# The last transformer stack of a fused kernel: the squared halves of each query and key head added on VectorE, half as many norm products on TensorE, and a new order of the stack's steps

## The chip, the cores and the metric

The kernel runs on one core of one Trainium2 chip. The metric is the device time of the whole kernel in microseconds, the median of several runs. The core's engines have short names in the profile: PE is TensorE, PEld its weight loads, DVE is VectorE, ACT is ScalarE, POOL is GpSimd, and SPq is the queue from which SyncE issues DMAs.

## The reference

The input is 16 sequences of 256 tokens with 128 features. Four blocks follow one another: an attention block with 16 heads, a mixture of low-rank experts, a retention block, and then a stack of six identical layers. The change touches the stack alone. One layer of it, with what matters for the change:

```
qkv = shift_tokens(x) @ Wqkv                     # 16 heads of 64
q = l2norm(q) * q_scale;  k = l2norm(k) * k_scale    # l2norm(t) = t / max(|t|, 1e-12)
q = q * cos * scale + rotate_half(q) * sin * scale   # k alike, with 1 / scale
out = local_attention(q, k, v)      # windows of 32 tokens, each sees itself and the one before
x = out @ Wo + x
x = feed_forward(shift_tokens(x)) + x     # layer norm, W1, a * gelu(gate), W2
```

The length |t| of a head needs the sum of 64 squares. The kernel holds a head as two halves of 32 features ("both parts of a head").

## The kernel before, in words

The work of the stack is cut into 96 units: unit u is layer u // 16 and sequence u % 16. The feed-forward block and what belongs to it (`fn`, `nat`, `st`, `rs`, `z`, `trf`, `fz`, `fg`, `gl`, `fa`, `fh`, `fy`, `xsf`) works on two sequences at once and so exists for even units alone. All data is float32.

One unit goes through these steps; the line is where the method begins. G counts four groups of four heads, k is 0 for queries and 1 for keys, and hu, tt and i count halves and quarters of the sequence or of the heads.

- `pqk.G.k` (L913, PE): two products of 128 by 256, the two halves of the heads, into a PSUM tile with two buffers (`ps_qk`).
- `sq.G.k` (L923, ACT) squares them into the SBUF tile `sq` of the group, which has four buffers. The tile is (128, k, half, 256).
- `t2.G.k` (L929) and `rot.G.k` (L934), both DVE, multiply the same PSUM tile by the rotary tables. `add.G` (L939, POOL) adds the two, 128 by 1024 elements.
- `nr` (L945, PE): the sums of squares. A fixed 0/1 matrix `gather` sums over the 32 features of a half in the partitions; the product runs over eight blocks b of 32 tokens, two halves hf, and four groups G, and accumulates the two halves in PSUM. In two parts of 32 products it makes 64 products for a unit. A float32 product is two instructions, so 128 matmul instructions.
- `rnA`, `rnB`, `rnC` (L961 to L968; DVE, ACT, DVE): maximum, square root, reciprocal.
- `bcD` (L973, SPq): one DMA stores the 128 by 64 result to DRAM, and eight more read it back, spread over the partitions, into the tile `bc` (one buffer).
- `norm.G` (L986, POOL): the group, 128 by 1024, times `bc`.
- `pv.i` (L991, PE), `vc.i` (L1002, ACT), `vs.tt` (L1005, SPq): the values, their copy out of PSUM, and four DMAs that copy them to a second place in SBUF. `vs.0` reads what `vc.0` and `vc.1` wrote, and `vs.1` what `vc.2` and `vc.3` wrote.
- `s.hu.tt.gh` (L1017, PE): scores of the groups G = 2 gh and 2 gh + 1. They lie in one PSUM tile (`ps_s`, one buffer) for the four steps of a hu; the next hu can be written once `sm.hu` has read it.
- `sm`, `mx` (DVE), `sub` (POOL), `exp` (ACT), `su`, `rec` (DVE): the softmax, L1043 to L1078.
- `pt`, `pTc`, `o`, `on`, `ot`, `oTc`, `y`, `xsu`: transposes, products with the values, and the output projection.

PSUM tiles of `pt`, `ot`, `pv`, `fg`, `fa`, `fn`, `trf`, `fy`, `y` and `nr` share one pool with two buffers (`misc`, L906): such a step waits until the tile two steps before it has been read.

The order of issue is written out by hand in the string `ORDER` (L1283). A word such as `norm.0:2` is a step and an offset d. The loop at L1343 runs a period j over all words and issues each for unit u = 2j + d where that unit exists. So a period holds every step twice, once for an even and once for an odd unit (feed-forward steps once); the 96 units make 48 periods, and a few more at both ends fill and empty the pipeline. Each engine works through its own steps strictly in this order, and so does SPq. Weights of the next layer are loaded by `follow` (L1315), which puts a DMA on SPq right behind the step that triggers it: the query and key weights of group G behind the second `pqk` of that group for sequence 15, the rotary tables behind the first `t2` of sequence 7, the value weights behind the first `pv` of sequence 9, the output weights behind the second `y` of sequence 15, the feed-forward weights behind `fy` of sequence 14. The query-key, output and feed-forward weights have one buffer, so that their DMA waits until that step has run. In the last layer `rs` also issues a DMA of the residual (`kept`), and `xsf` adds a transpose on PE, an addition on DVE and the DMA of the result.

Of the kernel before, what the change touches and what calls it, by code (L numbers as in the profile page):

```python
# [13 lines left out]
ALU = mybir.AluOpType  # L14
# [15 lines left out]
DEPTH, H2, D2, WIN = 6, 16, 64, 32  # L30
# [81 lines left out]
def kernel(ctx: ExitStack, tc: tile.TileContext, a: dict, widths: dict, out: bass.AP):  # L112
    nc = tc.nc
# [730 lines left out]
    gather = c["gather"].rearrange("p (b m) -> p b m", b=8)  # L844
# [43 lines left out]
    class Unit:  # L888
# [9 lines left out]
        def tile(self, pool, shape, what, *n, tag=None, **kw):  # L898

            key = (what, *n)  # L900
            if key not in self.tiles:
                name = f"{what}{self.u}_" + "".join(map(str, n))
                self.tiles[key] = pool.tile(shape, F32, tag=tag or what, name=name, **kw)
            return self.tiles[key]

# [35 lines left out]
            nc.gpsimd.tensor_tensor(to, to, self.t_2(G), ALU.add)  # L941

        def nr(self, part):  # L945
            nr = self.misc("nr")[:, 0:64]
            for b in range(4 * part, 4 * part + 4):
                for hf in range(2):
                    for G in range(4):
                        nc.tensor.matmul(  # L950
                            nr[32 * G : 32 * G + 32, :],
                            lhsT=gather[:, b, :],
                            rhs=self.squares(G)[:, :, hf, WIN * b : WIN * b + WIN],
                            start=(b == 0 and hf == 0),
                            stop=(b == 7 and hf == 1),
                        )

        def r_n(self):
            return self.tile(s2, [P, 64], "rn")
# [194 lines left out]
    class Forward(Unit):  # L1154
# [126 lines left out]


    ORDER = """  # L1283
        nr.0:2 t2.2.0:2 rot.2.1:2 y.1:-1 exp.1:0 sm.0:1 nr.1:2 t2.2.1:2 xsu:-1 pqk.0.1:3 add.3:2 rnA:2 rnB:2 pt.1.0:0
        s.1.0.0:1 su.1:0 rnC:2 add.2:2 rec.1:0 sq.0.1:3 fy:-4 s.1.1.0:1 mx.0:1 t2.0.1:3 rot.0.1:3 pqk.1.1:3 pTc.1.0:0
        sq.1.1:3 pt.1.1:0 o.0.0:0 xsf:-4 pqk.0.0:3 sub.0:1 pTc.1.1:0 fn:-2 t2.1.1:3 rot.1.1:3 t2.0.0:3 o.1.0:0 nat:-2
        exp.0:1 rot.0.0:3 bcD:2 pqk.1.0:3 add.0:3 on.0:0 sq.0.0:3 norm.0:2 pv.0:1 st:-2 s.1.1.1:1 norm.1:2 pv.3:1
        pqk.2.0:3 s.1.0.1:1 t2.1.0:3 vc.0:1 vc.3:1 ot.0.0:0 sq.1.0:3 pv.1:1 rot.1.0:3 rot.2.0:3 rs:-2 t2.2.0:3
        oTc.0.0:0 o.0.1:0 pt.0.0:1 sm.1:1 vc.1:1 sq.2.0:3 pqk.3.0:3 ot.0.1:0 sq.3.0:3 pTc.0.0:1 s.0.0.0:2 pqk.2.1:3
        z:-2 add.1:3 mx.1:1 trf:-2 rot.3.0:3 t2.3.0:3 oTc.0.1:0 su.0:1 sub.1:1 o.1.1:0 fz:-2 vs.0:1 pv.0:2 pqk.3.1:3  # L1290
        sq.2.1:3 on.1:0 t2.2.1:3 s.0.1.0:2 pv.3:2 vc.0:2 pt.0.1:1 norm.2:2 norm.3:2 exp.1:1 t2.3.1:3 vc.3:2 rot.2.1:3
        rot.3.1:3 vs.1:1 o.0.0:1 ot.1.0:0 oTc.1.0:0 rec.0:1 pTc.0.1:1 pqk.1.0:4 s.0.0.1:2 pt.1.0:1 add.2:3 su.1:1
        t2.1.0:4 sq.3.1:3 pqk.1.1:4 nr.0:3 pTc.1.0:1 nr.1:3 ot.1.1:0 rnA:3 rnB:3 rnC:3 fg.0:-2 bcD:3 sq.1.0:4
        oTc.1.1:0 gl.0:-2 s.0.1.1:2 sm.0:2 y.0:0 s.1.0.0:2 y.1:0 sq.1.1:4 s.1.1.0:2 xsu:0 rec.1:1 pt.1.1:1 pTc.1.1:1
        mx.0:2 rot.1.0:4 add.3:3 fa.0:-2 o.1.0:1 fg.1:-2 sub.0:2 t2.1.1:4 pqk.0.1:4 exp.0:2 fh.0:-2 rot.1.1:4
        s.1.0.1:2 t2.0.1:4 gl.1:-2 pv.1:2 pqk.3.1:4 on.0:1 s.1.1.1:2 ot.0.1:1 add.1:4 rot.0.1:4 vc.1:2 rot.3.1:4
        ot.0.0:1 sq.0.1:4 sq.3.1:4 oTc.0.1:1 norm.2:3 oTc.0.0:1 t2.3.1:4 pqk.0.0:4 sq.0.0:4 o.0.1:1 rot.0.0:4 norm.1:3
        sm.1:2 fa.1:-2 norm.3:3 pv.2:2 fh.1:-2 t2.0.0:4 o.1.1:1 pqk.3.0:4 sq.3.0:4 fg.2:-2 s.0.1.1:3 vc.2:2 norm.0:3
        gl.2:-2 vs.0:2 t2.3.0:4 on.1:1 pv.2:3 fa.2:-2 vc.2:3 s.0.0.1:3 add.0:4 pt.0.0:2 vs.1:2 fh.2:-2 pqk.2.0:4
        rot.3.0:4 ot.1.0:1 rot.2.0:4 pTc.0.0:2 oTc.1.0:1 su.0:2 s.0.0.0:3 rec.0:2 mx.1:2 sub.1:2 pqk.2.1:4 pt.0.1:2  # L1300
        ot.1.1:1 sq.2.1:4 pTc.0.1:2 s.0.1.0:3 y.0:1 sq.2.0:4 oTc.1.1:1
    """.split()

    weights = {}
# [4 lines left out]
    for word in ORDER:  # L1309
        name, d = word.split(":")  # L1310
# [105 lines left out]
```

## Time and profile before

| | |
|---|---|
| median of 3 runs | 4457.3 us (4455.6, 4457.3, 4475.08) |
| the profiled execution's own time | 4461.62 us |
| its span | 4459.9 us |
| busy in the span: PE, DVE, ACT, POOL | 4177.4, 2847.6, 2124.0, 2483.0 us |
| mean granted TensorE clock | 0.947 of full speed |

The profile is one execution. Busy shares are means over the whole span. The stack begins with its first weight load at 774 us and takes the rest. A stretch from one `fy` to the next is one period of the order, and the view of busy time by windows gives each engine's busy time in such a stretch. The timeline lists instructions in order of time: start, duration, engine, line, operation, what is written and read, the number of instructions merged into the row, and in brackets how long the engine stood idle before it and what released it.

### The profile page before, as it was taken

How to read it: one execution, taken by the hardware profiler on the slowest of the kernel's cores; microseconds unless marked ns; L12 is line 12 of the kernel's file. 1: busy time of each engine (PE TensorE's matmuls, PEld its weight loads, DVE VectorE, ACT ScalarE, POOL GpSimd, SP SyncE). 2: the span in 40 equal slices, each digit the busy share in tenths (PEclk: the TensorE clock that was granted, in tenths of full speed). 3: DMA queues.
4: the chain of work that ended last, by engine and by line, in shares of the span. 5: the costliest groups of instructions: out<-in, count | busy, mean ns of one | idle time of the engine just before them, and what ended most of it. 6: DMA issues, size and time to landing. Idle time of an engine off the chain costs nothing.

```text
span 4459.9 us, 219983 instructions
## 1 busy us (share of the span) xinstructions
PE 4177.4 (94%) x101856; PEld 2842.7 (64%) x101856; DVE 2847.6 (64%) x5628; ACT 2124.0 (48%) x3387; POOL 2483.0 (56%) x1419
## 2 busy tenths in 40 slices
PE   5888896799999999999999999999999999999998
PEld 3655664566666666666666666666666666666655
DVE  4555543567666666766667676766676766666664
ACT  2434432345555555545455455554555554544443
POOL 2433333666666666666666565665565665655552
PEclk9889876899999999999999999999999999999999
DMA  3200000222222222222222222222222222222221
GB/s 113 79 27 22 13 6 21 66 69 65 60 60 62 62 67 66 53 67 65 68 62 60 65 62 72 58 62 66 58 67 67 62 57 67 66 66 54 52 67 40
DMA packets 208917, 261.08 MB, mean 59 GB/s; under 512 B 54143, under 2 KB 164605, under 8 KB 207101
## 3 DMA queue, kind: packets, MB, share of 16 engines
q1 hardware_dynamic: 204796, 243.38, 22.1%
q8 instruction: 799, 13.09, 1.3%
q10 hardware_dynamic: 3200, 3.62, 0.3%
q14 instruction: 122, 0.99, 0.1%
HBM read 140.98 MB, written 17.83 MB: 36 GB/s over the span
## 4 chain that ended last, share of the span: by engine, by line
PE 81%; DVE 5%; issue 4%; DMA 3%; POOL 3%; SPq 2%; ACT 2%; ACTq 0%; POOLq 0%; DVEq 0%
PE pqk L916 15%; PE s L1028 12%; PE pv L994 8%; PE o L1104 6%; PE pt L1083 4%; PE ot L1129 4%; PE fa L1234 3%; PE fg L1221 3%; PE st L271 2%; SPq L981 2%; POOL qk L988 1%; PE sa L230 1%; PE or L537 1%; PE oa L306 1%; PE sr L510 1%
## 5 line engine op out<-in xcount | busy, mean ns | idle before, releaser
L941 POOL TENSOR_TENSOR qk<-qk,t 128x1024 f32<-128x1024 f32 x384 | 907.2, 2373 | 307.0 <-DVE qk L935 208.8
L1059 POOL TENSOR_TENSOR sm<-sm,mx 128x1024 f32<-128x1024 f32 x192 | 365.1, 1902 | 1005.8 <-DVE mx L1055 711.3
L916 PE MATMUL pqk<-xs,wqk 128*128 128x256 f32 x3072 | 861.3, 404 | 15.7 <-DVE qk L935 4.6
L1028 PEld LDWEIGHTS s<-qk 32*32 32x32 f32 x49152 | 535.4, 104 | 407.4 <-issue 334.6
L924 ACT ACTIVATE sq<-pqk 128x512 f32<-128x512 f32 x768 | 459.7, 599 | 631.6 <-PE pqk L916 543.4
L1028 PE MATMUL s<-qk 32*32 32x64 f32 x49152 | 666.4, 224 | 69.0 <-POOL qk L988 59.7
L930 DVE TENSOR_TENSOR t<-pqk,rot 128x512 f32<-128x512 f32 x768 | 522.5, 684 | 275.0 <-ACT sq L924 136.7
L916 PEld LDWEIGHTS pqk<-xs,wqk 128*128 128x128 f32 x3072 | 538.4, 194 | 246.3 <-issue 87.3
L935 DVE TENSOR_TENSOR qk<-pqk,rot 128x512 f32<-128x512 f32 x768 | 516.9, 683 | 268.1 <-PE s L1028 137.5
L994 PE MATMUL pv<-wv,xs 128*64 128x512 f32 x1536 | 429.4, 638 | 0.0
L1091 ACT COPY pT<-pt 128x512 f32<-128x512 f32 x384 | 224.4, 584 | 375.6 <-PE pt L1083 337.3
L1104 PEld LDWEIGHTS o<-v,pT 64*32 64x32 f32 x24576 | 273.1, 107 | 173.5 <-issue 161.9
L1104 PE MATMUL o<-v,pT 64*32 64x64 f32 x24576 | 339.6, 227 | 7.8 <-issue 5.5
L1003 ACT COPY v<-pv 128x512 f32<-128x512 f32 x384 | 223.9, 583 | 239.6 <-PE pv L994 239.4
L1044 DVE TENSOR_TENSOR sm<-s,c_ident 128x1024 f32<-128x1024 f32 x192 | 233.6, 1217 | 58.2 <-PE s L1028 58.2
L286 POOL TENSOR_SCALAR_AFFINE_SELECT pe<-pe 128x512 f32<-128x512 f32 x128 | 81.6, 638 | 328.1 <-ACT pe L279 311.6
L1083 PE MATMUL pt<-c_ident,sm 128*128 128x128 f32 x1536 | 244.8, 282 | 0.8 <-ACT oT__71843 L1135 0.8
L1129 PE MATMUL ot<-c_ident,on 128*128 128x128 f32 x1536 | 234.0, 280 | 1.4 <-ACT f_gl L1227 0.8
L1067 DVE TENSOR_REDUCE su<-sm 128x16 f32<-128x1024 f32 x192 | 230.1, 1198 | 1.5
L1063 ACT ACTIVATE sm<-sm 128x1024 f32<-128x1024 f32 x192 | 203.3, 1059 | 57.1 <-POOL sm L1059 56.0
L1055 DVE TENSOR_REDUCE mx<-sm 128x16 f32<-128x1024 f32 x192 | 226.0, 1177 | 0.1
L242 DVE CUSTOM_DVE_ANT_0 junk<-sa,c_mask 128x128 f32<-128x128 f32 (+1 forms) x512 | 181.9, 355 | 64.6 <-PE sa L230 31.5
(2243 smaller groups left out, 6740.9 us busy)
## 6 DMA issues: line engine op xcount, KB each, us to landing
v<-v SPq DMA_DIRECT2D x576, 128.0 KB
v<-v SPq DMA_DIRECT2D x192, 64.0 KB
rot_l<-in_rot_dram SPq DMA_DIRECT2D x12, 512.0 KB
rot<-rot_l SPq DMA_DIRECT2D x12, 512.0 KB
wqk<-in_wqk_dram SPq DMA_DIRECT2D x24, 256.0 KB
rot<-rot SPq DMA_DIRECT2D x6, 1024.0 KB
wv<-in_wv_dram SPq DMA_DIRECT2D x6, 512.0 KB
wo<-in_wo_dram SPq DMA_DIRECT2D x6, 512.0 KB
```

Source lines behind the costliest of these rows:

```text
L916: nc.tensor.matmul(self.p_qk(G, k)[:, hf, :], lhsT=weights["qk", G, self.l][:, k, hf, :], rhs=xq, start=True, stop=True)
L924: nc.scalar.activation(self.squares(G)[:, k], self.p_qk(G, k), AF.Square)
L930: nc.vector.tensor_tensor(self.t_2(G)[:, k], self.p_qk(G, k)[:, ::-1, :], weights["rot", self.l][:, 1, k], ALU.mult)
L935: nc.vector.tensor_tensor(self.qk_t[G][:, k, :, WIN : WIN + T], self.p_qk(G, k), weights["rot", self.l][:, 0, k], ALU.mult)
L941: nc.gpsimd.tensor_tensor(to, to, self.t_2(G), ALU.add)
L994: nc.tensor.matmul(self.misc("pv", i)[64 * p : 64 * p + 64, :], lhsT=xs[self.g][:, self.s, cols], rhs=weights["v", self.l][:, p, :], start ...
L1028: nc.tensor.matmul(ps[32 * b : 32 * b + 32, r2, tt, G // 2, G % 2, :], lhsT=qk[G][rows, 0, hf, WIN + at : 2 * WIN + at], rhs=keys, start=( ...
L1044: nc.vector.tensor_tensor(self.t_sm(hu).rearrange("n r t g p c -> n r (t g p c)"), self.p_s(hu).rearrange("n r t g p c -> n r (t g p c)"), ...
L1059: nc.gpsimd.tensor_tensor(s3, s3, self.t_mx(hu)[:, :, None].to_broadcast([P, 16, 2 * WIN]), ALU.subtract)
L1083: nc.tensor.transpose(pt[:, j * P : (j + 1) * P], sm[:, j // 2, tt, j % 2].rearrange("n p c -> n (p c)"), ident)
L1104: nc.tensor.matmul(o[WIN * b : WIN * b + WIN, p, 4 * hu + j, :], lhsT=pT[rows, at : at + WIN], rhs=self.v_t[rows, 1 - b % 2, 2 * tt + b // ...
L1129: nc.tensor.transpose(ot[:, m * P : (m + 1) * P], on[:, p, m, :], ident)
```

## The change

A new step `ps.G` on DVE adds, in place, the second half's squares to the first half's for queries and keys at once: 128 by 512 elements, both inputs and the output in SBUF. `nr` then reads the first half alone, makes 32 products for a unit where there were 64, and makes them in one run where there were two steps of half the length. In the order the two `nr` steps of a unit are replaced by one, four `ps` steps come in, and the whole string is new: every step keeps its work, and its place and offset can differ. A third edit puts an underscore into tile names and changes nothing else.

```
@@ -941,19 +941,23 @@
             nc.gpsimd.tensor_tensor(to, to, self.t_2(G), ALU.add)
-        def nr(self, part):
+        def ps(self, G):
+            sq = self.squares(G)
+            nc.vector.tensor_tensor(sq[:, :, 0], sq[:, :, 0], sq[:, :, 1], ALU.add)
+        def nr(self, _):
             nr = self.misc("nr")[:, 0:64]
-            for b in range(4 * part, 4 * part + 4):
-                for hf in range(2):
-                    for G in range(4):
-                        nc.tensor.matmul(
-                            nr[32 * G : 32 * G + 32, :],
-                            lhsT=gather[:, b, :],
-                            rhs=self.squares(G)[:, :, hf, WIN * b : WIN * b + WIN],
-                            start=(b == 0 and hf == 0),
-                            stop=(b == 7 and hf == 1),
-                        )
+            for b in range(8):
+                for G in range(4):
+                    nc.tensor.matmul(
+                        nr[32 * G : 32 * G + 32, :],
+                        lhsT=gather[:, b, :],
+                        rhs=self.squares(G)[:, :, 0, WIN * b : WIN * b + WIN],
+                        start=(b == 0),
+                        stop=(b == 7),
+                    )
         def r_n(self):
             return self.tile(s2, [P, 64], "rn")
@@ -1281,24 +1285,24 @@
     ORDER = """
-        nr.0:2 t2.2.0:2 rot.2.1:2 y.1:-1 exp.1:0 sm.0:1 nr.1:2 t2.2.1:2 xsu:-1 pqk.0.1:3 add.3:2 rnA:2 rnB:2 pt.1.0:0
-        s.1.0.0:1 su.1:0 rnC:2 add.2:2 rec.1:0 sq.0.1:3 fy:-4 s.1.1.0:1 mx.0:1 t2.0.1:3 rot.0.1:3 pqk.1.1:3 pTc.1.0:0
-        sq.1.1:3 pt.1.1:0 o.0.0:0 xsf:-4 pqk.0.0:3 sub.0:1 pTc.1.1:0 fn:-2 t2.1.1:3 rot.1.1:3 t2.0.0:3 o.1.0:0 nat:-2
-        exp.0:1 rot.0.0:3 bcD:2 pqk.1.0:3 add.0:3 on.0:0 sq.0.0:3 norm.0:2 pv.0:1 st:-2 s.1.1.1:1 norm.1:2 pv.3:1
-        pqk.2.0:3 s.1.0.1:1 t2.1.0:3 vc.0:1 vc.3:1 ot.0.0:0 sq.1.0:3 pv.1:1 rot.1.0:3 rot.2.0:3 rs:-2 t2.2.0:3
-        oTc.0.0:0 o.0.1:0 pt.0.0:1 sm.1:1 vc.1:1 sq.2.0:3 pqk.3.0:3 ot.0.1:0 sq.3.0:3 pTc.0.0:1 s.0.0.0:2 pqk.2.1:3
-        z:-2 add.1:3 mx.1:1 trf:-2 rot.3.0:3 t2.3.0:3 oTc.0.1:0 su.0:1 sub.1:1 o.1.1:0 fz:-2 vs.0:1 pv.0:2 pqk.3.1:3
-        sq.2.1:3 on.1:0 t2.2.1:3 s.0.1.0:2 pv.3:2 vc.0:2 pt.0.1:1 norm.2:2 norm.3:2 exp.1:1 t2.3.1:3 vc.3:2 rot.2.1:3
-        rot.3.1:3 vs.1:1 o.0.0:1 ot.1.0:0 oTc.1.0:0 rec.0:1 pTc.0.1:1 pqk.1.0:4 s.0.0.1:2 pt.1.0:1 add.2:3 su.1:1
-        t2.1.0:4 sq.3.1:3 pqk.1.1:4 nr.0:3 pTc.1.0:1 nr.1:3 ot.1.1:0 rnA:3 rnB:3 rnC:3 fg.0:-2 bcD:3 sq.1.0:4
-        oTc.1.1:0 gl.0:-2 s.0.1.1:2 sm.0:2 y.0:0 s.1.0.0:2 y.1:0 sq.1.1:4 s.1.1.0:2 xsu:0 rec.1:1 pt.1.1:1 pTc.1.1:1
-        mx.0:2 rot.1.0:4 add.3:3 fa.0:-2 o.1.0:1 fg.1:-2 sub.0:2 t2.1.1:4 pqk.0.1:4 exp.0:2 fh.0:-2 rot.1.1:4
-        s.1.0.1:2 t2.0.1:4 gl.1:-2 pv.1:2 pqk.3.1:4 on.0:1 s.1.1.1:2 ot.0.1:1 add.1:4 rot.0.1:4 vc.1:2 rot.3.1:4
-        ot.0.0:1 sq.0.1:4 sq.3.1:4 oTc.0.1:1 norm.2:3 oTc.0.0:1 t2.3.1:4 pqk.0.0:4 sq.0.0:4 o.0.1:1 rot.0.0:4 norm.1:3
-        sm.1:2 fa.1:-2 norm.3:3 pv.2:2 fh.1:-2 t2.0.0:4 o.1.1:1 pqk.3.0:4 sq.3.0:4 fg.2:-2 s.0.1.1:3 vc.2:2 norm.0:3
-        gl.2:-2 vs.0:2 t2.3.0:4 on.1:1 pv.2:3 fa.2:-2 vc.2:3 s.0.0.1:3 add.0:4 pt.0.0:2 vs.1:2 fh.2:-2 pqk.2.0:4
-        rot.3.0:4 ot.1.0:1 rot.2.0:4 pTc.0.0:2 oTc.1.0:1 su.0:2 s.0.0.0:3 rec.0:2 mx.1:2 sub.1:2 pqk.2.1:4 pt.0.1:2
-        ot.1.1:1 sq.2.1:4 pTc.0.1:2 s.0.1.0:3 y.0:1 sq.2.0:4 oTc.1.1:1
+        sq.1.1:3 sm.1:1 o.1.1:0 nat:-2 mx.1:1 exp.0:1 pqk.2.0:3 rot.2.1:3 rot.2.0:3 ot.0.1:0 norm.0:2 oTc.0.1:0
+        sq.2.1:3 sub.1:1 norm.2:2 pv.0:2 t2.2.0:3 s.0.0.0:2 exp.1:1 sq.2.0:3 t2.2.1:3 fy:-4 vc.0:2 st:-2 s.0.1.0:2
+        su.0:1 pqk.3.1:3 pv.0:1 norm.3:2 s.0.1.1:2 xsf:-4 pqk.3.0:3 rs:-2 vc.0:1 rot.3.1:3 rec.0:1 pv.3:2 sq.3.1:3
+        sq.3.0:3 vc.3:2 ps.1:3 pt.0.0:1 z:-2 s.0.0.1:2 pTc.0.0:1 add.1:3 ps.3:3 trf:-2 pt.0.1:1 add.2:3 t2.3.0:3
+        t2.3.1:3 pqk.1.1:4 ps.2:3 rot.3.0:3 fz:-2 nr.0:3 sm.0:2 pTc.0.1:1 rnA:3 pt.1.0:1 fg.0:-2 s.1.0.0:2 rnB:3
+        pTc.1.0:1 pv.1:2 on.1:0 rnC:3 su.1:1 gl.0:-2 vc.1:2 pqk.1.0:4 mx.0:2 vs.0:1 o.0.0:1 t2.1.0:4 ot.1.0:0 fa.0:-2
+        s.1.1.0:2 t2.1.1:4 oTc.1.0:0 fh.0:-2 ot.1.1:0 sq.1.1:4 add.3:3 rec.1:1 fg.1:-2 vs.0:2 oTc.1.1:0 rot.1.1:4
+        s.1.1.1:2 vs.1:1 gl.1:-2 rot.1.0:4 pqk.3.0:4 add.1:4 sub.0:2 pt.1.1:1 o.1.0:1 sq.1.0:4 on.0:1 y.0:0 sq.3.0:4
+        s.1.0.1:2 y.1:0 bcD:3 t2.3.0:4 pTc.1.1:1 sm.1:2 o.0.1:1 pqk.0.1:4 ot.0.1:1 mx.1:2 xsu:0 ot.0.0:1 exp.0:2
+        rot.3.0:4 norm.0:3 rot.0.1:4 norm.1:3 o.1.1:1 oTc.0.0:1 su.0:2 norm.3:3 ps.1:4 norm.2:3 oTc.0.1:1 t2.0.1:4
+        sq.0.1:4 pqk.0.0:4 t2.0.0:4 fa.1:-2 s.0.0.0:3 pqk.3.1:4 rot.0.0:4 fh.1:-2 sq.0.0:4 pv.2:2 vc.2:2 s.0.1.0:3
+        rec.0:2 rot.3.1:4 pt.0.0:2 sq.3.1:4 sub.1:2 on.1:1 t2.3.1:4 pt.0.1:2 pTc.0.0:2 pqk.2.1:4 s.0.0.1:3 fg.2:-2
+        pTc.0.1:2 ps.3:4 exp.1:2 ps.0:4 pqk.2.0:4 sq.2.1:4 add.3:4 su.1:2 s.0.1.1:3 gl.2:-2 rot.2.1:4 sq.2.0:4 add.0:4
+        pt.1.0:2 t2.2.1:4 sm.0:3 t2.2.0:4 ot.1.1:1 pqk.0.1:5 s.1.0.0:3 ps.2:4 rot.2.0:4 pTc.1.0:2 oTc.1.1:1 rec.1:2
+        pv.2:3 pqk.0.0:5 vc.2:3 mx.0:3 t2.0.0:5 nr.0:4 rnA:4 t2.0.1:5 fa.2:-2 sub.0:3 fh.2:-2 ot.1.0:1 rnB:4 oTc.1.0:1
+        s.1.1.0:3 rnC:4 pv.1:3 sq.0.0:5 sq.0.1:5 o.0.0:2 vc.1:3 rot.0.0:5 y.0:1 s.1.1.1:3 rot.0.1:5 y.1:1 xsu:1
+        add.2:4 o.1.0:2 pqk.1.0:5 pqk.1.1:5 on.0:2 vs.1:2 rot.1.0:5 rot.1.1:5 o.0.1:2 ot.0.0:2 bcD:4 add.0:5 t2.1.0:5
+        pv.3:3 t2.1.1:5 ps.0:5 sq.1.0:5 oTc.0.0:2 s.1.0.1:3 vc.3:3 pt.1.1:2 fn:0 norm.1:4 pTc.1.1:2 pqk.2.1:5
     """.split()
     weights = {}
```

More of the change, by code (lines that the diff above doesn't have):

```diff
@@ L901, in tile @@
             if key not in self.tiles:
-                name = f"{what}{self.u}_" + "".join(map(str, n))
+                name = "_".join([f"{what}{self.u}", *map(str, n)])
                 self.tiles[key] = pool.tile(shape, F32, tag=tag or what, name=name, **kw)
```

## The prediction

> **What bounds the kernel now.** I read the page's busy times first, then busy time by windows from one `fy` to the next (one period of ORDER), then the timeline of each engine inside one period.
>
> ```profile
> span 4459.9 us, 219983 instructions
> PE 4177.4 (94%) x101856; PEld 2842.7 (64%) x101856; DVE 2847.6 (64%) x5628; ACT 2124.0 (48%) x3387; POOL 2483.0 (56%) x1419
> ```
> ```profile
> core 0: us, PE busy (x) PEld busy (x) DVE busy (x) ACT busy (x) POOL busy (x), PEclk, DMA share, GB/s
> 1291.50:1374.50 83.00, 76.81 (x2011) 51.20 (x2011) 50.77 (x83) 38.25 (x58) 45.84 (x21) 0.94 0.25 64
> 1599.00:1671.60 72.60, 72.58 (x2011) 49.48 (x2011) 50.59 (x83) 38.35 (x58) 45.95 (x21) 1.00 0.26 59
> 3985.90:4067.30 81.40, 76.51 (x2015) 51.45 (x2015) 51.16 (x84) 38.35 (x58) 45.86 (x21) 0.94 0.24 59
> ```
> An ordinary period lasts 72.6 us and PE is busy for all of it; DVE has 22 us to spare, POOL 27. Three kinds of period are longer: where query-key weights are reloaded (83.0), where feed-forward weights are (1520.3 to 1599.0: 78.7), and five in the last layer (403.5 us together, 40 more than five ordinary ones). What happens in the first kind:
>
> ```profile
> 1298.43 0.36 SPq L859 DMA_DIRECT2D wqk<-in_wqk_dram  x1
> 1298.88 1.17 SPq L975 DMA_DIRECT2D ndr<-rn__16289  x1
> ...
> 1310.48 4.64 POOL L988 TENSOR_TENSOR qk<-qk,bc__16480 128x1024 f32<-128x1024 f32 x2 [8.22 <-DMA wqk<-in_wqk_dram]
> ...
> 1312.88 0.46 PE L1028 MATMUL s<-qk 32*32 32x64 f32 x32 [3.27 <-POOL qk L988]
> ```
> The chain `rnC`, SPq, two DMA trips, `norm`, `s` came late, since SPq stood at the weight load; PE waited and then ran at a lower clock. In an ordinary period the same chain is on time:
>
> ```profile
> 1598.70 0.38 SPq L975 DMA_DIRECT2D ndr<-rn__21696  x1
> 1600.36 4.43 SPq L981 DMA_DIRECT2D bc__21887<-ndr  x8
> ...
> 1610.15 4.69 POOL L988 TENSOR_TENSOR qk<-qk,bc__21887 128x1024 f32<-128x1024 f32 x2 [0.42 <-POOL qk L941]
> ```
> From store to `norm` 11.45 us, though nothing was in the way; 11.25 at 1524.02 and 9.1 at 799.33.
>
> [...] `z`, issued while POOL adds, has one instruction of 2371 ns, where its fellows take 334.
>
> ```profile
> 1614.79 1.02 POOL L1186 TENSOR_TENSOR rs__21909<-rs__21909,mhalf 128x4 f32<-128x4 f32 x1
> 1615.78 2.35 POOL L941 TENSOR_TENSOR qk<-qk,t 128x1024 f32<-128x1024 f32 x1
> ```
> ```profile
> 1615.85 3.14 DVE L1196 TENSOR_SCALAR ln_z__22100<-f_nat__21882,ln_mv__21908,rs__21909 128x128 f32<-128x128 f32 x4 [0.47 <-POOL rs__21909 L1186]
> ```
> No DVE instruction of the stack before has two SBUF tensor inputs; `ps` will be the first. [...] the trace's 684 (L930, one input in PSUM) is close. [...] after 3.27 and 1.84 us of waiting a `pqk` took 2.08 us, not 1.13.
>
> **The change, part by part.** I use positions: the start-to-start distances of PE steps (from ordinary timelines) added up along ORDER. They are pqk 0.96 to 1.06, s 0.785, pv 1.01, o 0.79, pt and ot 0.43 to 0.58, y 1.92, fa 1.02, fg 0.96, fy 2.77. The old order gives 72.4 against 72.6 measured, so the method holds.
>
> 1. Fewer products.
>
> ```profile
> 1665.29 1.10 PE L950 MATMUL nr__22964<-sq,c_ident 128*32 128x64 f32 x64
> 1666.32 1.99 PE L1142 MATMUL y__22957<-oT__22669,wo 128*128 128x256 f32 x8
> 1668.24 1.10 PE L950 MATMUL nr__22964<-sq,c_ident 128*32 128x64 f32 x64
> 1669.27 1.13 PE L916 MATMUL pqk<-xs,wqk 128*128 128x256 f32 x4
> ...
> 1702.34 2.00 PE L950 MATMUL nr__23661<-sq,c_ident 128*32 128x64 f32 x128
> 1704.27 0.66 PE L1129 MATMUL ot<-c_ident,on 128*128 128x128 f32 x4
> ```
> A run of 64 instructions costs 1.03 us, one of 128 1.93: 1.03 + 1.03 + 1.93 = 3.99 a period. Two runs of 64 will cost 2.06. With the new neighbours the new order adds up to 70.6: 1.8 us less, times 48 = **-87 us**, if PE stays fed.
>
> 2. `ps`: 8 a period at 0.69 us = 5.5 us on DVE (51 to 56.6 of 70.6). That fits, so the bare work costs nothing; what costs is where it stands and whom it locks out. POOL is busy for 46 of 72.6 us, with instructions of 1.9 to 2.4 us, so a `ps` at a random moment waits 0.63 x 1.15 = 0.7 us, up to 2.4.
>
> 3. First tight place: DVE from `sm.1:1` to `ps.2:3`. `sm.1:1` can start at 69.1 (after `pt.1.1:2`, whose buffer it takes over); `nr.0:3` is due at 70.6 + 15.8 = 86.4: 17.3 us. In between, in order, DVE must do sm 1.2, mx 1.2, two rot and two t2 2.7, st 2.0, su 1.2, xsf 1.5, rot 0.7, rec 0.3, ps 0.7, z 1.3, ps 0.7, two t2 1.4, ps 0.7: 15.6, and 0.6 of waiting for `pqk.2.0`. That leaves 1.1 us. POOL in that stretch does norm, sub, norm, norm, rs and then two adds back to back, at about 81 to 85.5, just where ps.1, z and ps.3 stand. `z` alone loses 2.0 as now, one more lock 1 to 2.4. Stall: 15.6 + 0.6 + 2.0 + 1.6 - 17.3 = 2.5 us. Bounds 0 (they miss each other) and 4.4 (each add goes first). Behind it wait trf, pqk.1.1:4 (needs t2.3.1) and nr. I take **2.5**.
>
> 4. Second tight place: SPq. `bcD:3` now stands behind `vs.0:2` and `vs.1:1`, and `vs.0:2` waits for `vc.1:2`, copy of `pv.1:2`, which ends at 20.1 (`rnC:3` is ready at about the same time). Before, `bcD` had no unready `vs` before it. SPq does wait in order:
>
> ```profile
> SPq L1010 <- ACT v L1003: 435.6, 67, 11.2
> ```
> The chain: `rnB`, `pTc`, `gl.0` and `vc.1` on ACT 1.4 after pv; eight `vs` DMAs at 0.6 = 4.8; store to norm 10.5; four norms 9.4; sub.1 1.9; exp.1 1.1; su.1 1.2; rot and t2 1.4; sm.0:3 1.2; handoffs 0.6: 33.5 us. PE has 50.1 - 20.1 = 30.0 us of work until `s.1.0.0:3`, which needs the PSUM tile that sm.0:3 reads; pt.1.0:2 needs exp.1 and pqk.0.1:5 needs that t2. Stall **3.5**. Bounds: 1.1 (ACT free, DMA 9.1) and 7 (DMA 11.5, and ps.1, ps.3, ps.0 each getting in front of a norm). The even unit: rnC:4 at 57.5, + 10.5, two norms 4.7 = 72.7 against `s.0.0.0:2` at 73.8: just in time, nothing.
>
> 5. Weight loads and moved DMAs. Calibration: the store of `bcD` comes 0.2 us before `fy` in an ordinary period; 4.0 us late it cost 6.1 (feed-forward weights), 7.6 late 10.4 (query-key): 16.5 a layer change, 82 for five. New: the feed-forward loads come at 6.8 and bcD:3 at 27, so that cost goes. The G=1 load stands behind pqk.1.1:5 (65.4), then vs.1:2, then bcD:4: store at 68.3, not 57.5, so 10.8 late, some 14 us. The output-weight load waits for y.1:1 (62.7), again before vs.1:2 and bcD:4: 8 late, some 11. 25 x 5 = 125: **+43**. Rotary and value loads have a free second buffer and don't block. In the last layer the result's DMA and `kept` now pass SPq before 18, ahead of the vs that bcD:3 waits for anyway: of the 40 us I count **-35**.
>
> 6. Neutral: ACT loads tables 6 times a period, not 7; the largest offset is 5, not 4, worth under 10 us at the ends.
>
> Sum: I count 43 full periods: 43 x (2.5 + 3.5) = +258. -87 + 258 + 43 - 35 = +179. Against the profiled execution's 4461.6: 4641; the median lies 4.3 lower: **4637 us**, 4.0% slower. What is late next: with PE stalled, nothing else is full; the cycle runs through SPq, POOL and DVE.
>
> **The rivals.** (Time that the measurement can tell from no change: 0.5%, 22 us.)
>
> A. The DVE-POOL lock hardly binds and only the SPq chain stalls: 43 x 3.5 = 150; -87 + 150 + 43 - 35 = +71: **4528**. For: no run here shows the lock for two SBUF inputs. Against: `z` shows it for its kind.
>
> B. Both chains near their upper ends plus half clock after each stall, 9 us a period: -87 + 387 + 43 - 35 = +308: **4765**. For: the 3.27 us wait above cost 10 in all.
>
> C. The other side: PE stays fed. If `vs` and `bcD` come at the low ends and the locks fall into DVE's idle time, a period takes 70.6 to 71.6, so -79 to -36: **4378 to 4421**. Deciding point: 1.8 us of stall a period eat the gain, less with item 5. For: DVE and POOL have spare time on average, and before, no stall remained in an ordinary period. Against: DVE's 1.1 us of slack holds no single lock.
>
> **How the numbers follow.** Forecast 0.30, A 0.26, B 0.16, C 0.22, and 0.06 between C and A, within 0.5%. So faster 0.22, same 0.06, slower 0.72. The range cuts C at 4390 and B at 4765: about half of each is outside, 0.19. Cases of both signs are inside, so it is wide; the forecast's own range is 4570 to 4700.
>
> **What would show it.** nr at 32 products a unit, 2.06 us a period. `ps` with a minimum near 0.69 us and single ones of 2 to 3 beside a POOL instruction. Periods near 76.6 with PE busy below 72, waits of `trf`, `pqk` or `nr` for DVE, of `s` for POOL norm and of `s` or `pqk` for DVE `sm` or `t`. SPq at L1010 waiting for ACT ahead of L975. Wrong if ordinary periods show PE busy throughout at about 70.6, or if `ps` never exceeds 0.7 us.

## The result, and the profile after

The kernel after takes **4798.1 us** (median of 4 runs, 4780.2 to 4801.5), the kernel before beside it 4458.9: a ratio of 1.075, 95% interval 1.072 to 1.078. The forecast, 4637, had the direction and both stalls, but its range ended at 4765: the loss is nearly twice what was summed up.

The head of the page of after, which answers to the first fence of before:

```profile
span 4799.8 us, 207615 instructions
PE 4232.8 (88%) x95712; PEld 2803.2 (58%) x95712; DVE 3310.1 (69%) x6012; ACT 2073.5 (43%) x3342; POOL 2558.8 (53%) x1419
```

PE executes 6,144 matmuls fewer and is busy for 55 us **more**. Span less PE's busy time is 567.0 us, before 282.5. So of the 340 us between the two spans 284.5 are idle PE and 55.4 busy PE. The mean granted clock fell from 0.947 to 0.921.

Where PE stands idle, from the waits of PE in after (what PE waited for; us in total, times, longest us):

```profile
PE s L1032 <- POOL qk L992: 214.5, 109, 5.1
PE pqk L916 <- DVE t L930: 84.4, 87, 3.5
PE trf L1206 <- DVE ln_z L1200: 35.3, 42, 2.0
PE o L1108 <- DMA v<-v: 34.1, 16, 4.5
```

Before, the first of these was 59.7 us in 26 waits, and `pqk` waited for DVE's rotations 4.6 us in 6. Below stands an ordinary period of after, in the same views that the prediction used for before: its row in the busy time by windows, and the rows that matter from the timelines of PE, of SPq, of DVE, and of ACT and POOL. "..." marks rows left out.

```profile
core 0: us, PE busy (x) PEld busy (x) DVE busy (x) ACT busy (x) POOL busy (x), PEclk, DMA share, GB/s
1781.20:1860.20 79.00, 72.78 (x1895) 48.02 (x1882) 61.92 (x91) 36.86 (x58) 47.49 (x22) 0.98 0.25 60
```
```profile
1792.05 1.01 PE L1206 MATMUL trf<-c_ident,ln_z 128*128 128x128 f32 x4 [0.87 <-DVE ln_z L1200]
...
1794.54 1.13 PE L916 MATMUL pqk<-xs,wqk 128*128 128x256 f32 x4 [1.04 <-DVE t L930]
1795.60 1.10 PE L954 MATMUL nr<-sq,c_ident 128*32 128x64 f32 x64
1796.63 0.66 PE L1087 MATMUL pt<-c_ident,sm 128*128 128x128 f32 x4
...
1820.24 0.46 PE L1032 MATMUL s<-qk 32*32 32x64 f32 x32 [1.62 <-POOL qk L992]
1822.54 0.46 PE L1032 MATMUL s<-qk 32*32 32x64 f32 x32 [1.84 <-POOL qk L992]
1822.93 2.01 PE L916 MATMUL pqk<-xs,wqk 128*128 128x256 f32 x4
...
1834.76 1.10 PE L916 MATMUL pqk<-xs,wqk 128*128 128x256 f32 x4 [0.85 <-DVE t L930]
```
```profile
1787.62 19.02 SPq L1014 DMA_DIRECT2D v<-v  x12
1806.74 0.53 SPq L979 DMA_DIRECT2D ndr<-rn  x1
1808.54 4.23 SPq L985 DMA_DIRECT2D bc<-ndr  x8
```
```profile
1783.25 2.35 DVE L1186 TENSOR_SCALAR rs<-ln_mv 128x4 f32<-128x4 f32 x1
...
1789.52 3.16 DVE L1200 TENSOR_SCALAR ln_z<-f_nat,ln_mv,rs 128x128 f32<-128x128 f32 x4
1792.60 0.68 DVE L946 TENSOR_TENSOR sq<-sq 128x512 f32<-128x512 f32 x1
...
1798.04 0.54 DVE L972 RECIPROCAL rn<-rn 128x64 f32<-128x64 f32 x1
...
1852.98 2.70 DVE L946 TENSOR_TENSOR sq<-sq 128x512 f32<-128x512 f32 x1
```
```profile
1800.01 0.59 ACT L1007 COPY v<-pv 128x512 f32<-128x512 f32 x1
```
```profile
1780.88 4.69 POOL L992 TENSOR_TENSOR qk<-qk,bc 128x1024 f32<-128x1024 f32 x2
...
1817.83 9.28 POOL L992 TENSOR_TENSOR qk<-qk,bc 128x1024 f32<-128x1024 f32 x4 [7.91 <-DMA bc<-ndr]
...
1852.77 5.16 POOL L992 TENSOR_TENSOR qk<-qk,bc 128x1024 f32<-128x1024 f32 x2 [6.58 <-DMA bc<-ndr]
```

How to read it. `nr` costs 1.03 us from start to start, as forecast. `rnC` (L972) ends at 1798.6, but SPq issues the store (L979) at 1806.74, 8.2 us later: the `vs` DMAs (L1014, merged into one row) stand ahead of it. The first `norm` starts at 1817.83. The two halves of one `s` step, `s.0.0.0:3`, then wait for the norms of their two groups, 1.62 and 1.84 us. The `pqk` behind takes 2.01 us where others take 1.13; the granted clock was 0.76 from 1822 to 1824 us and 0.50 from 1824 to 1826. Waits of 0.2 us and more come to 6.2 us, PE's work to 72.8 where the positions gave 70.6.

The lock of step 3, DVE and POOL instructions that hold each other up, is there too. In the view of the tile `sq` (minimum/median/maximum in ns, first and last start):

```profile
L946 DVE TENSOR_TENSOR sq<-sq x384: 637/681/2877, 788.8 to 4673.6; 128x512 f32<-128x512 f32 x192
```

The mean is 1242 ns. Of the 384 `ps`, 141 take more than 0.8 us, and every one of these ends 0.55 us after an instruction of POOL does (within 0.03 us): it waits for POOL, and then does its own work. The `ps` at 1852.98 is one, held up by the norm that began at 1852.77. It works the other way too: an add or a norm beside a `ps` that came first takes up to 2.9 us, where the longest in before took 2.43.

### The profile page after: what moved, and what is told of

Its sections match the earlier page's. It is cut to its first block, busy times and chain, and to the rows that moved or that the text cites. A ratio compares the mean times of both kernels' runs of the same rounds, so it can differ in the third digit from the quotient of the medians.

```text
span 4799.8 us, 207615 instructions
## 1 busy us (share of the span) xinstructions
PE 4232.8 (88%) x95712; PEld 2803.2 (58%) x95712; DVE 3310.1 (69%) x6012; ACT 2073.5 (43%) x3342; POOL 2558.8 (53%) x1419
## 4 chain that ended last, share of the span: by engine, by line
PE 46%; DVE 21%; SPq 8%; DMA 7%; POOL 6%; issue 6%; ACT 6%; POOLq 0%; ACTq 0%; DVEq 0%
PE pqk L916 8%; PE pv L998 6%; PE s L1032 6%; DVE sq L946 5%; PE y L1146 4%; POOL qk L992 4%; DMA bc<-ndr 4%; SPq L985 4%; SPq L1014 3%; DVE t L930 3%; PE o L1108 3%; PE nr L954 2%; DMA ndr<-rn 2%; PE st L271 2%; DVE ln_z L1200 2%
## 5 line engine op out<-in xcount | busy, mean ns | idle before, releaser
L992 POOL TENSOR_TENSOR qk<-qk,bc 128x1024 f32<-128x1024 f32 x384 | 913.6, 2407 | 818.6 <-DMA bc<-ndr 753.5
L941 POOL TENSOR_TENSOR qk<-qk,t 128x1024 f32<-128x1024 f32 x384 | 962.6, 2517 | 618.3 <-DVE qk L935 412.5
L916 PE MATMUL pqk<-xs,wqk 128*128 128x256 f32 x3072 | 900.5, 421 | 102.7 <-DVE t L930 84.4
L1032 PE MATMUL s<-qk 32*32 32x64 f32 x49152 | 678.1, 228 | 214.8 <-POOL qk L992 214.5
L916 PEld LDWEIGHTS pqk<-xs,wqk 128*128 128x128 f32 x3072 | 560.1, 200 | 315.7 <-issue 101.6
L930 DVE TENSOR_TENSOR t<-pqk,rot 128x512 f32<-128x512 f32 x768 | 507.6, 682 | 114.7 <-ACT sq L924 75.9
L946 DVE TENSOR_TENSOR sq<-sq 128x512 f32<-128x512 f32 x384 | 473.2, 1242 | 2.4 <-ACT sq L924 2.4
L998 PE MATMUL pv<-wv,xs 128*64 128x512 f32 x1536 | 465.1, 687 | 0.0
L1139 ACT COPY oT<-ot 128x512 f32<-128x512 f32 x384 | 219.6, 585 | 485.6 <-PE ot L1133 485.5
L1146 PE MATMUL y<-oT,wo 128*128 128x256 f32 x1536 | 382.4, 392 | 0.7 <-ACT oT L1139 0.7
L1121 DVE TENSOR_TENSOR on<-o,rec 128x1024 f32<-128x1024 f32 x192 | 234.0, 1219 | 155.1 <-PE o L1108 153.6
L1146 PEld LDWEIGHTS y<-oT,wo 128*128 128x128 f32 x1536 | 276.1, 189 | 48.2 <-ACT oT L1139 0.9
```

What stands on the lines that cost most here:

```text
L916: nc.tensor.matmul(self.p_qk(G, k)[:, hf, :], lhsT=weights["qk", G, self.l][:, k, hf, :], rhs=xq, start=True, stop=True)
L930: nc.vector.tensor_tensor(self.t_2(G)[:, k], self.p_qk(G, k)[:, ::-1, :], weights["rot", self.l][:, 1, k], ALU.mult)
L946: nc.vector.tensor_tensor(sq[:, :, 0], sq[:, :, 0], sq[:, :, 1], ALU.add)
L992: nc.gpsimd.tensor_tensor(to, to, self.bcast()[:, G, :, None, :].to_broadcast([P, 2, 2, T]), ALU.mult)
L998: nc.tensor.matmul(self.misc("pv", i)[64 * p : 64 * p + 64, :], lhsT=xs[self.g][:, self.s, cols], rhs=weights["v", self.l][:, p, :], start ...
L1032: nc.tensor.matmul(ps[32 * b : 32 * b + 32, r2, tt, G // 2, G % 2, :], lhsT=qk[G][rows, 0, hf, WIN + at : 2 * WIN + at], rhs=keys, start=( ...
```

## The experiments

All ran on one core, in batches, each beside runs of the kernel before. Its median was 4448 to 4458 us from batch to batch, so that a difference of two kernels of different batches is good to some 10 us. "Ordinary" is the median distance from `fy` to `fy` without those at layer changes; the last column is span less PE's busy time. The two kernels with one SBUF input (nolock) leave out the sum itself.

| kernel | order, sum | median us | ratio to before, 95% | ordinary us | PE busy us | rest us |
|---|---|---|---|---|---|---|
| before | old, none | 4458.9 | 1 | 72.7 | 4177.4 | 282.5 |
| after | new, `ps` | 4798.1 | 1.072 to 1.078 | 79.1 | 4232.8 | 567.0 |
| a_bcd3 | new, one store early | 4584.8 | 1.025 to 1.032 | 75.8 | 4158.2 | 439.8 |
| a_bcd34 | new, both stores early | 4487.6 | 1.005 to 1.009 | 75.1 | 4116.0 | 369.2 |
| a_nops | new, none | 4762.7 | 1.066 to 1.072 | 79.4 | 4270.9 | 478.7 |
| a_nolock | new, one SBUF input | 4694.6 | 1.053 to 1.058 | 78.0 | 4207.8 | 487.8 |
| a_bcd34_nolock | both stores early, one input | 4343.0 | 0.973 to 0.978 | 72.3 | 4071.5 | 271.4 |
| a_bcd34_nops | both stores early, none | 4392.1 | 0.984 to 0.990 | 73.6 | 4138.1 | 248.2 |
| b_ps | old, `ps` | 4532.1 | 1.015 to 1.020 | 74.3 | 4099.8 | 410.0 |
| b_bcd2 | old with one store early, none | 4344.8 | 0.974 to 0.982 | 72.6 | 4117.2 | 216.8 |
| b_ps_bcd2 | the same, `ps` | 4449.8 | 0.999 to 1.001 | 74.3 | 4101.4 | 362.6 |
| b_bcd2_red | the same, sum by a reduce | 4312.7 | 0.967 to 0.971 | 72.0 | 4057.9 | 260.2 |
| a_bcd34_red | both stores early, a reduce | 4430.0 | 0.993 to 0.997 | 74.2 | 4102.9 | 315.4 |
| b_bcd2_red_nr | b_bcd2_red, `nr.0:3` later | 4311.8 | 0.966 to 0.969 | 71.9 | 4043.6 | 278.5 |

**The late stores.** Theory: `bcD` behind unready `vs` is the larger stall. Rival: the lock on DVE. a_bcd3 moves two words, a_bcd34 two more:

```
- ... vs.0:1 o.0.0:1 ... s.1.1.1:2 vs.1:1 gl.1:-2 ... y.1:0 bcD:3 t2.3.0:4 ...
+ ... vs.0:1 vs.1:1 bcD:3 o.0.0:1 ...                        (a_bcd3)
- ... rnC:4 pv.1:3 ... on.0:2 vs.1:2 rot.1.0:5 ... ot.0.0:2 bcD:4 ...
+ ... vc.2:2 vs.1:2 ... rnC:4 bcD:4 pv.1:3 ...               (a_bcd34 as well)
```

> The changed kernel with three words of its order moved: vs.1:1 and bcD:3 right behind vs.0:1, so that bcD:3 no longer waits on SPq for vc.1:2. Theory 1 (two separate stalls a period, SPq chain about 4.3 us of waiting plus 2.2 us of lower clock, DVE-POOL lock about 1.9 us): the SPq part goes, ordinary periods fall from 78.8 to 72.5 to 73.5 us, time 4480 to 4560, and the waits of trf and pqk for DVE (0.9 and 1.0 us a period) stay. Rival (the lock behind ps is the cause and SPq only shows it): under 1.5 us a period, time over 4720.

> As the one before, and vs.1:2 right behind vc.2:2 and bcD:4 right behind rnC:4, ahead of the weight loads of sequence 15. Theory 1: ordinary periods as in the one before, and the two long periods of a layer change (88.7 and 87.5 us) come down to ordinary ones, 18 us a layer, 90 for five: 4390 to 4470. Rival (long periods come from the weights themselves arriving late for pqk or y): no difference to the one before.

a_bcd3 gives back 213 us (the ordinary period 3.3 of its 6.4), a_bcd34 97 more: the distances at layer changes lose their surplus (22.3 us a layer in after, 21.0 in a_bcd3, 0.4 here), as step 5 had it. Both came out above their ranges, a_bcd3 by 25 us and a_bcd34 by 18: the ordinary period fell to 75.8 and 75.1 us, not to 72.5 to 73.5. With both stores early PE waits for DVE and ACT; its waits for norms, 214.5 us in after, are down to 10.5 in 6 waits:

```profile
PE pqk L916 <- DVE t L930: 75.9, 94, 3.5
PE pqk L916 <- ACT sq L924: 47.4, 40, 2.1
PE trf L1206 <- DVE ln_z L1200: 37.2, 45, 2.0
```

**The order alone, the arithmetic alone.** a_nops drops the eight `ps` words (four for each of two units) and lets `nr` take both halves, in one run of 64 products; b_ps puts the eight `ps` and the short `nr` into the old order (`ps.0:3` behind `t2.1.0:3`, `ps.1:3` behind `sm.1:1`, `nr.0:3` behind `ot.1.1:0`, and so on).

> The new order alone: ps is left out and nr makes all 64 products of a unit in one run. PE has 0.9 us more for each unit. Theory 1: the lock stalls go (1.9 us a period), the SPq stall stays and is somewhat smaller, since the norms aren't interrupted: ordinary periods 76 to 78 us, time 4670 to 4760. Rival (the added DVE work and its lock are the cause, the order is fine): ordinary periods near 72.5, time near 4450.

> The old order with the new arithmetic alone: ps put in behind the squares, nr with 32 products in one run at or just behind the place of the old second part. Theory 1: the arithmetic is sound and the order did the harm. PE saves 1.93 us a period; DVE has 22 us to spare, needs 5.5 for ps and some 5 for the lock: ordinary periods 70.8 to 72, time 4365 to 4430. Rival (the lock costs wherever ps stands): no gain or a loss, 4460 to 4650.

The order alone does most of the harm: 4762.7, just above its range, with 205.2 us of `s` waiting for norm. My theory for b_ps fell, and the rival written beside it held: `ps` costs in the old order too. DVE's `ps` there has a median of 924 ns, and `nr` waits for it 49 times:

```profile
PE nr L954 <- DVE sq L946: 72.7, 49, 2.9
PE s L1032 <- POOL qk L992: 60.4, 29, 4.5
```

**The lock by itself.** The same step, place and number, but a reduction with one SBUF input. That this kind takes no lock was assumed; in after `su`, a reduction of 1024 elements with one such input, took 1.16 to 1.22 us in each of its 192 instructions:

```
-            nc.vector.tensor_tensor(sq[:, :, 0], sq[:, :, 0], sq[:, :, 1], ALU.add)
+            nc.vector.tensor_reduce(sq[:, :, 0, 0:1], sq[:, :, 1], AX.X, ALU.add)
```

> The changed kernel with ps as a reduction over one SBUF input of 512 elements (two results per partition, written where nr reads, so that nr still waits for it): the same place and about the same DVE time, no second SBUF input. It leaves out the addition of the second halves, so the norms are others. Theory 1: waits of trf and pqk for DVE shrink by about half (z keeps its own lock), the SPq stall stays: 2 to 3 us a period, time 4650 to 4710. Rival (the lock is all): near 4450. Rival (no lock for two SBUF inputs): no change, 4790.

> The same replacement in the kernel with bcD and vs moved (4488 us). There PE waits 1.6 us a period for t, 1.0 for sq and 0.8 for z. Theory 1: with the lock of ps gone ordinary periods fall from 74.9 to 71.5 to 73, time 4330 to 4410. Rival (what is left comes from the order, not the lock): within 20 us of 4488. It leaves out the same addition.

> bcD and vs moved, ps left out, nr with all 64 products in one run: the new order repaired, with the old arithmetic. PE needs 72.5 us a period. If the arithmetic (ps and half the products) is a gain once the order is right, this is slower than 4488; theory 1 says that ps costs more than the 1.9 us that it saves on PE (4.3 us of stall a period are left with it), so this one is at 72.6 to 73.5 a period, 4380 to 4430.

All three fell inside their ranges. The tile `sq` of a_bcd34_nolock shows the twin of the row above. It reads 512 elements from one input and writes two results, and all 384 lie within 59 ns of one another. So POOL held up none of them, and the long `ps` of after are due to the lock.

```profile
L946 DVE TENSOR_REDUCE sq<-sq x384: 630/676/689, 786.4 to 4230.1; 128x2 f32<-128x512 f32 x192
```

The lock costs 104 us while the stores are late (4798.1 to 4694.6) and 145 once they are early (4487.6 to 4343.0). What `ps` does as written, against `nr` over both halves, is 4487.6 - 4392.1 = 95 us of loss; a sum as short as this reduction and without the lock would gain 49.

**The old order and its one late store.** In before, `bcD:2` too stands behind the weight loads.

```
- ... s.1.0.0:1 su.1:0 rnC:2 add.2:2 ... exp.0:1 rot.0.0:3 bcD:2 pqk.1.0:3 ...
+ ... s.1.0.0:1 su.1:0 rnC:2 bcD:2 add.2:2 ... exp.0:1 rot.0.0:3 pqk.1.0:3 ...
```

> The old kernel with one word moved: bcD:2 right behind rnC:2, ahead of the feed-forward and query-key weight loads and of the last layer's result DMA on SPq. Theory 1 (a store behind a DMA that waits is what makes the long periods): 83.0, 78.7 and the last layer's 81 all fall to about 72.7, 82 + 40 less: 4335 to 4370. Rival (the traffic of the loads itself is the cause): less than 40 us gained.

> The order of before with ps as changed (in place, two SBUF inputs) and the short nr placed in it, and in it bcD:2 moved right behind rnC:2. If the late store and the lock are separate costs, the move gives back what it gave without ps (about 4450 to 4345, 105 us): 4532 - 105 = 4427, range 4400 to 4450, and ordinary periods stay at 74.2 while the long ones at the layer changes go. Theory lock-anywhere: still above the 4345 of the same order without ps, by 60 us or more. If the long waits of nr for ps came from the same late store: 4365 or less, so that ps pays after all.

One word is worth 104 us: the surplus at a layer change falls from 15.5 to 1.7 us and that of the last layer's five periods from 37.1 to -2.7, so 5 x 13.8 + 39.8 = 109. With `ps` (b_ps_bcd2) it is 82 us, which gives the time of before; the median `ps` has grown to 1474 ns, and 247 of the 384 are over 0.8 us, where b_ps had 220. Against b_bcd2 `ps` loses 105 us. Both runs came out inside their ranges.

Held beside a_bcd34_nops of the same batch, b_bcd2 shows what the new order is worth. Both do the old arithmetic and both have their stores early: the new order takes 4392.1 us, the old one 4344.8. So the new order is not merely spoilt by its late stores; it is 47 us slower without them too.

**A sum without the lock.** `ps` as one reduce over the two halves, written where dead data lies (the second half of the group before), with `nr` reading from there (not shown: the list `sums`, `nr`'s new input, and one buffer for `ln_z`, which makes room):

```
-            nc.vector.tensor_tensor(sq[:, :, 0], sq[:, :, 0], sq[:, :, 1], ALU.add)
+            to = self.squares(list(self.sums)[-1])[:, :, 1] if self.sums else self.tile(s2, [P, 2, T], "qs", bufs=1)
+            nc.vector.tensor_reduce(to, sq.rearrange("p k h t -> p k t h"), AX.X, ALU.add)
+            self.sums[G] = to
```

> As b_ps_bcd2, but ps is one tensor_reduce over the two halves (1024 elements in from one SBUF tile, 512 out, 128 partitions) that writes into the second half of the squares of the group before, whose own sum has been taken (the first group of a unit into a small tile of its own; ln_z gets one buffer to make room for it). All of the reference is computed. [...] ps should take about 1.2 us with minimum and maximum close together (su, a reduce of 1024 elements, takes 1198 ns). DVE then has 8 x 1.2 = 9.6 us of ps a period, 60 of 71 us. Lock theory: the long single ps go and PE is fed, about 70.8 to 71.5 a period: 4345 - 48 x (1.2 to 1.9) = 4255 to 4290; with some new lateness on DVE up to 4340. Rival, that DVE's mere work is what is too much: above 4345, near b_ps_bcd2 or over it.

> The new order with bcD:3, bcD:4 and the two vs moved (as a_bcd34), and ps as the same tensor_reduce. All of the reference is computed. Against the 4343 of the same order with the short one-input ps (676 ns) each ps is 0.5 us longer, and three of them stand in the tight stretch of DVE ahead of nr.0:3: up to 1.6 us a period, 0 to 75 us: 4345 to 4420, most likely 4375. Rival, that the tight stretch is only made so by the lock and has room without it: 4343 or less. If the lock were not the cause but ps's length, it would be at or over the 4488 of a_bcd34, since the mean of ps is there 1.24 us too.

```profile
L948 DVE TENSOR_REDUCE sq<-sq x288: 1214/1231/1256, 793.0 to 4210.0; 128x512 f32<-128x1024 f32 x144
```

Nearly twice the 0.68 us of an unblocked `ps`, but always the same. In the old order it is 32 us faster than b_bcd2 and 3.1% faster than before, less than the 4255 to 4290 that I thought likely. In the new order it comes out 10 us above its range and takes 38 us more than no sum at all (a_bcd34_nops): `pqk` waits for `t` 75.3 us there, against 21.1. That fits step 3, which had found 1.1 us of slack on DVE ahead of `nr.0:3`; three `ps` of 1.23 us in that stretch add 1.6. The page's head of b_bcd2_red, to be held against that of after:

```profile
span 4318.1 us, 207995 instructions
PE 4057.9 (94%) x95712; PEld 2750.9 (64%) x95712; DVE 3244.7 (75%) x6012; ACT 2130.4 (49%) x3387; POOL 2486.2 (58%) x1419
```

The last run took aim at its remaining waits, of `nr` for `ps` and of `fg` for `rnA`:

```
- ... ot.1.1:0 nr.0:3 rnA:3 rnB:3 rnC:3 fg.0:-2 bcD:3 sq.1.0:4 oTc.1.1:0 gl.0:-2 s.0.1.1:2 sm.0:2 y.0:0 ...
+ ... ot.1.1:0 fg.0:-2 sq.1.0:4 oTc.1.1:0 gl.0:-2 s.0.1.1:2 nr.0:3 sm.0:2 rnA:3 rnB:3 rnC:3 bcD:3 y.0:0 ...
```

> As b_bcd2_red, and nr.0:3 moved back by two PE steps, behind s.0.1.1:2, with rnA:3, rnB:3, rnC:3 and bcD:3 behind sm.0:2. All of the reference is computed. In an ordinary period of b_bcd2_red PE is busy 70.7 of 72.0 us; between 2000 and 3000 us nr waited 12 times for ps, 0.46 us each, and fg 14 times 0.3 us for rnA, which reads the PSUM tile ahead of it. The move gives ps.3:3 1.7 us more, and fg comes before nr. If these waits are what is left: 0.7 to 0.9 a period, 33 to 43 us, 4270 to 4280, with something new late up to 4300. Rival, that the later store of unit 3 makes norm late in its place: 4313 or more, with waits of s for POOL norm.

The gain did not come: 4311.8, no change that could be measured. The rival's waits of `s` for norms are there but small, 11.4 us where b_bcd2_red has 4.7. `nr` waits for `ps` 6.5 us now (25.4 before the move) and `fg` for `rnA` no more (14.6), but a new wait has their size. With `nr` between, `y.0` takes over the PSUM buffer of `fg`, and waits until ACT has read it (`gl`):

```profile
PE y L1149 <- ACT f_gl L1234: 38.0, 45, 0.9
```

## Why the prediction was right in direction and wrong in size

**The step that failed is the term of step 1: "-87 us, if PE stays fed".** The forecast says in steps 3 and 4 that PE does not stay fed, and yet kept PE's work at the length of a fed PE. The lower clock after a stall went into rival B and, through its calibration in elapsed time, into step 5, but not into the stalls of the ordinary periods. Measured over the whole span: idle +284.5 us against +266 forecast (258 + 43 - 35), busy +55.4 against -87. That is 18 and 142 of the 161 us that are missing. In the 45 periods from the first `fy` on, idle grew by 258 us, which is about what the stalls were forecast at, and busy by 45, where 45 x -1.8 = -81 was expected; the rest is at the ends (point 6).

That it is the clock, and not the work, is seen in three kernels with the new order and the same 95,712 matmuls: PE was busy for 4232.8 us with 567.0 idle at a mean granted clock of 0.921 (after), 4116.0 with 369.2 at 0.945 (a_bcd34), 4071.5 with 271.4 at 0.955 (a_bcd34_nolock). From end to end that is 161.3 / 295.6: in this order each us of idle PE cost another 0.55. The price is no constant. In the old order, with as many matmuls, b_ps has PE busy for 4099.8 us with 410.0 idle and b_bcd2_red 4057.9 with 260.2: 41.9 / 149.8, or 0.28. What sets it was not tried. In the trace of after the low clock comes behind the two waits of 1.62 and 1.84 us, 0.5 us of work between them: 0.76 and then 0.50 granted, and a `pqk` of 2.01 us. Behind the single waits of 0.87 and 1.04 us in the same period the granted clock was 1.00 (1792 to 1798 us). In before it was 0.50 from 1316 to 1324 us, behind 3.27 and 1.84 us of waiting.

Point by point:

1. *Fewer products.* Right as work: runs of 64 at 1.03 us, and a nearly fed period of the new arithmetic, in the old order, has PE busy for 70.8 of 72.0 us (b_bcd2_red). As a term of the sum it failed, as above.
2. *`ps` at 0.69 us.* 0.68 where nothing blocks it (L930, with as many elements and one input in PSUM, took 0.684 in before), and 0.56 more on average; 0.7 was estimated for a random moment. Right. That POOL would hold it up was the author's assumption: the trace of before has no such instruction in the stack.
3. *First tight place, 2.5 us.* Mechanism right: `z` blocked by an add (3.16 us for its four, which take 1.10 where POOL is idle), then `trf` waiting 0.87 and `pqk` 1.04, 1.9 us in the period shown, against 2.5. The lock of all eight `ps` together, with the clock that it costs, is 145 us over 43 periods or 3.4 each; how much of that belongs to this place was not tried. The lock alone gives 104, which fits that part of it hides behind the late store.
4. *Second tight place, 3.5 us.* The cause is right, the store behind `vs`, and the size near: 1.62 + 1.84 + 0.85 = 4.3 in the period shown. The place is not the one forecast. The chain was followed through the softmax to `s.1.0.0:3`, which did not wait in this period. PE waited earlier, at `s.0.0.0:3`, which reads the norms themselves, and then 0.85 us at `pqk.0.1:5`. That the size came out near is luck in part. Too small were the eight `vs` (6.1 us from the end of `vc.1` at 1800.6 to the store, not 4.8) and store to norm (11.1, not 10.5). The 11.45 us that the prediction read "though nothing was in the way" had an add of POOL up to 0.42 us before the norm, so POOL may have had a part in it. The even unit's store, counted at nothing in an ordinary period, was worth at most 0.7 us, together with `vs.1:2` (75.8 to 75.1).
5. *Loads.* 22.3 us a layer change (predicted 25), before 15.5: 5 x 6.8 = 34 us against 43. Last layer: 37.1 us over five ordinary periods before, -0.6 after: -38 against -35. Right.
6. *Ends, "under 10 us".* Wrong. The first `fy` comes at 1047.3 us, before at 999.6, with the first `sq` at 782.9 and 783.6; the last two distances are 10.7 us shorter together: +37. Part of it is the stalls again; from the first `sq` to the first `fy` it is 264.4 us in after, 242.2 in a_bcd34_nolock and 216.0 before. That the remaining 26 come from the offset 5 is argued, not tried.

Rival B had the mechanism that was missing, though not after each stall as it says, and is the nearest case. Rival A fell (the lock costs 104 to 145 us). Rival C, PE fed, is nearly what a_bcd34_nolock shows, 4343 with both stalls taken away, but that kernel leaves out the sum. With a sum that works and takes no lock (a_bcd34_red) the new order is only 0.5% faster than before, and the old order with the same sum (b_bcd2_red) 3.1%.

## What to carry to other kernels

When a sum of stalls is made for a kernel bound by PE, price PE's work at the clock that it will have with these stalls: here each us of waiting cost 0.28 to 0.55 us more. In an order written by hand, put a small DMA whose data is ready ahead of larger ones whose data isn't, and look at weight loads on the same queue: one word moved was worth 104 us here, and the halved products with the best sum found another 32. Where a stretch of DVE has little slack and POOL is busy, reckon a DVE operation like `ps` at its longest (2.9 us in after, not 0.68). A reduce of twice the elements with one input took 1.21 to 1.26 us every time and was the cheaper one in the whole kernel.

## What was not expected of the hardware

- A DVE tensor_scalar of 128 by 4 (`rs`, at 1783.25 in the period shown) took 2.35 us, and 0.17 at 1609.98 in before. POOL ran two norms from 1780.88 to 1785.57, and `rs` ended with the second of them, within 0.03 us. So four elements in each partition can be held up as long as many: `rs` took 2.36 us at most, `z` with its 128 elements 2.40.
- A tensor_reduce of 1024 to 512 elements with a stride of 256 between the two that it adds takes 1.23 us, hardly more than one that reads 1024 elements into 16 (1.20).
- Taking a wait away can leave the time as it is where PSUM has two buffers for ten kinds of tile: 33.5 us of waits for `ps` and `rnA` went, 38.0 for `gl` came.
